# Side products in the banks of the score pairs, in an attention and block-quantized feed-forward kernel

## The chip, the cores and the metric

The kernel runs on one core of one Trainium2 chip. The metric is the device time of one execution in microseconds (us). The core has five engines, each with a queue of its own that it works off in order: TensorE (PE; its weight loads are listed apart as PEld), VectorE (DVE), ScalarE (ACT), GpSimd (POOL) and SyncE (SP), which here only starts DMAs. TensorE writes its results into PSUM[...], and ScalarE or VectorE read them from there.

## The reference

`x` is 4 x 1024 x 256, the context is 4 x 77 x 256, both float32. One attention block and one feed-forward block, each with a layer norm ahead and a residual around it:

```python
# attention: 16 heads of 16; keys and values from the context followed by x itself
q = x @ Wq
xc = concatenate((mem, x), axis=1)
k, v = split(xc @ Wkv, 2, axis=-1)
dots = einsum('bhid,bhjd->bhij', q, k) * scale
mask = j_idx > i_idx + mem_len            # causal behind the 77 context keys
attn = softmax(where(mask, -inf, dots), axis=-1)
out = einsum('bhij,bhjd->bhid', attn, v) @ Wout + bout
# feed-forward: both operands of both products rounded in blocks of 32
def block_quant(v):                       # exponent from the block's largest magnitude, 3 bits
    e = floor(log2(max(amax, tiny)))
    scale = exp2(e - 3)
    return round(vb / scale) * scale
h = gelu(einsum('bsk,nk->bsn', block_quant(x), block_quant(w_fc)) + b_fc)    # 1024 hidden
y = einsum('bsk,nk->bsn', block_quant(h), block_quant(w_proj)) + b_proj
# whole
x = x + attention(layernorm(x), ctx);  x = x + feed_forward(layernorm(x))
```

## The kernel before

**Groups, steps and half steps.** The 4 batches have 16 heads, taken in groups of 4, so there are 16 groups (`kk`). For one group the scores are computed twice. The first time gives, for each query row, the maximum over its keys (`max_matmul`, L451, then `max_reduce` on DVE, L475 or L477). The maxima are carried by DMA into a spare row of the queries, so that the second time the product is the score less its maximum (`score_matmul`, L515). The exponential on ACT (`score_exp`, L526) reads it from PSUM and writes `pt`; POOL clears what the causal mask forbids (L531), and `times_v` (L552) multiplies by V, summing into one bank of its own.

The maxima of group `kk + 1` run beside the scores of group `kk`. A group has 14 pieces (key tile by query stretch of up to 512), each done in two half steps for two heads each. A half step (`half_step`) issues on PE: maximum of head 1, score of head 1, maximum of head 2, score of head 2. These lie in four different row groups of the PE array, 32 rows each. The text calls the two maxima of a half step the first and the second. Then come two reductions on DVE and one exponential for the pair of scores on ACT. `times_v` follows for a piece two steps back, four matmuls for each half step. There are 448 half steps, and ahead of them 14 steps (`first_step`) in which the maxima of group 0 are computed alone, four heads at a time.

**Side work.** All else is cut into units which `run` puts between the half steps: layer norm and transposes of the next batch (`norm_unit`, L324; `mem_unit`, L343), projections to V (`v_unit`, L359) and to Q and K (`qk_unit`, L386), output product of attention (`wout_unit`, L642 and its bias L646), the two feed-forward products with their transposes (`in_unit`, L683; `hidden_unit`, L702 and L707; `out_unit`, L736, L744 and L747), and the quantized weights, transposed (`weight_unit`, L771). Each unit has a cost written by hand; `run` spreads the sum of the costs over the half steps and begins a unit when its share is due. Its later stages come some half steps after. The order of all instructions is fixed in this way when the program is built (`tc.manual_schedule()`); the engines keep to it and wait for each other by semaphores.

A side product, as the text uses the word, is one PSUM tile written by one of these units other than `hidden_unit`. ACT reads most of them (copies); the two output products (L642, L744) are read by DVE, which adds them to the residual (L647, L748). There are 256 of them, 198 of them after 75 us and before 1067 us.

**PSUM.** Tiles of a pool take its slots in turn, in order of allocation. A tile's first write waits until the last read of the tile that had its slot before has ended.

```python
ps_st = ap("ps_st", 2, space=PSUM)   # score pairs: 2 slots of two banks
ps_av = ap("ps_av", 1, space=PSUM)   # products with V: 1 bank
ps_s = ap("ps_s", 3, space=PSUM)     # s_tile: 3 banks
```

Score pairs (both scores of a half step, one tile) and the hidden products take `ps_st`; maxima and side products take `ps_s` together through `s_tile`. In `first_step` two of four maxima take `ps_s`, the other two a pair of `ps_st`.

**Ahead and behind.** Until about 75 us the first batch is normed and projected and group 0's maxima are found. From there to 1067 us the half steps run. After that come the last batch's output product (its second half) and its feed-forward, with no scores beside them.

Of the kernel before, what the change touches and what calls it, by code (L numbers as in the profile page):

```python
# [9 lines left out]
F32 = mybir.dt.float32  # L10
# [33 lines left out]
def kernel(  # L44
# [158 lines left out]
    with ExitStack() as actx:  # L203
# [52 lines left out]
        def s_tile(shape, dtype=F32):  # L256
            return ps_s.tile(shape, dtype, tag="s", name="s_ps")

        xT, o_pk, sums = {}, {}, {}


# [42 lines left out]
        def norm_unit(b, it):  # L304
            t = b * NT + it
            got = {}

            def scale_rows():
                held["xh"] += 1
                xh = work.tile([P, D], F32, name="xh")  # L310
                nc.vector.tensor_scalar(
                    xh, xn[b, it // HN][:, it % HN, :], mv1[:, t, 0:1], rstd1[:, t : t + 1],
                    ALU.subtract, ALU.mult,
                )
                got["xh"] = xh

            def turn():
                if it == 0:

                    assert b == 0 or projected[b - 1] == 2 * KC  # L320
                    xT[b] = xtp.tile([P, KC, KEYS], F32, name="xT")
                tp = s_tile([P, KC, P])
                for k in range(KC):
                    nc.tensor.transpose(tp[:, k, :], got["xh"][:, k * P : (k + 1) * P], ident)  # L324
                held["xh"] -= 1
                nc.scalar.copy(xT[b][:, :, M + it * P : M + (it + 1) * P], tp)
                normed[b] += 1

            scale_rows.ready = room("xh", XH)
            return cost(0.8, [scale_rows, turn])  # L330

        def mem_unit(b):
            got = {}

            def fetch():
                held["xh"] += 1
                got["m"] = work.tile([P, D], F32, name="xh")
                nc.sync.dma_start(out=got["m"][:M, :], in_=mem[b])

            def turn():  # L340
                tp = s_tile([P, KC, M])
                for k in range(KC):
                    nc.tensor.transpose(  # L343
                        tp[:, k, :], got["m"][:M, k * P : (k + 1) * P], ident[0:M, 0:M]
                    )
                held["xh"] -= 1
                nc.scalar.copy(xT[b][:, :, 0:M], tp)  # L347
                normed[b] += 1

            fetch.ready = room("xh", XH)  # L350
            return cost(0.5, [fetch, turn])

        def v_unit(b, jt):
            def emit():
                assert normed[b] == NT + 1
                nj = min(P, KEYS - jt * P)
                vp = s_tile([P, D])
                for k in range(KC):
                    nc.tensor.matmul(  # L359
                        vp[:nj, :], xT[b][:, k, jt * P : jt * P + nj], wv[:, k, :],  # L360
                        start=(k == 0), stop=(k == KC - 1),
                    )
                base = vaugs[b % 2][:nj, jt, :]
                nc.scalar.copy(
                    bass.AP(
                        base.tensor, base.offset,
                        [base.ap[0], [VP, HPC], [VOFF[1], 2], [2, HD]],
                    ),
                    vp[:nj, :].rearrange("p (q e d) -> p q e d", e=2, d=HD),
                )  # L370
            return emit

        def qk_unit(hh, which, part):

            def emit():
                b, hi = divmod(hh, KC)
                assert normed[b] == NT + 1
                if which == "q":
                    w, first, total = wq_sb, M, N
                else:  # L380
                    w, first, total = wk_sb, 0, KEYS
                lo = part * ICW
                n = min(ICW, total - lo)
                pp = s_tile([P, ICW])
                for k in range(KC):
                    nc.tensor.matmul(  # L386
                        pp[:, :n],
                        w[:, k, hi * P : (hi + 1) * P],
                        xT[b][:, k, first + lo : first + lo + n],
                        start=(k == 0),  # L390
                        stop=(k == KC - 1),
                    )
                nc.scalar.copy(qk_st[:, lo : lo + n], pp[:, :n])  # L393
                projected[b] += lo + n == total
            return cost(1.0, emit)
# [235 lines left out]
        def wout_unit(b, it):  # L631
            t = b * NT + it
            ic = it * P // ICW

            def fetch():
                x2[t] = xrp.tile([P, D], F32, name="x2")
                nc.sync.dma_start(out=x2[t], in_=xf[t * P : (t + 1) * P, :])

            def project():
                yp = s_tile([P, D])  # L640
                for k in range(KC):
                    nc.tensor.matmul(  # L642
                        yp, o_pk[b, ic][:, k, it * P % ICW : it * P % ICW + P], wo_sb[:, k, :],
                        start=(k == 0), stop=False,
                    )
                nc.tensor.matmul(yp, ones3, bias3[:, B_OUT : B_OUT + D], start=False, stop=True)  # L646
                nc.vector.tensor_add(x2[t], x2[t], yp)  # L647
                stats(x2[t], mv2, t)
                done["wout"] += 1

            fetch.ready = lambda: (b, ic) in divided and len(x2) - done["out"] < X2
            return cost(1.8, [fetch, project])
# [14 lines left out]
        def in_unit(t):  # L667
            got = {}

            def quantize():  # L670
                done["begun"] += 1
                held["xq"] += 1
                xh = work.tile([P, D], F32, name="xh")
                nc.vector.tensor_scalar(
                    xh, x2[t], mv2[:, t, 0:1], rstd2[:, t : t + 1], ALU.subtract, ALU.mult
                )
                got["xq"] = ffn.tile([P, D], BF16, name="xq", bufs=XQ)
                quant_round(xh, quant_steps(xh, D, "x"), got["xq"])

            def turn():  # L680
                tp = s_tile([P, KC, P], BF16)
                for k in range(KC):
                    nc.tensor.transpose(tp[:, k, :], got["xq"][:, k * P : (k + 1) * P], identb)  # L683
                held["xq"] -= 1
                xqT[t] = ffn.tile([P, KC, P], BF16, name="xqT", bufs=HBUF + 1)
                nc.scalar.copy(xqT[t], tp)  # L686

            quantize.ready = lambda: (
                t // HN in rooted and done["begun"] - len(hs) <= HBUF
                and held["xq"] < XQ and held["xh"] < XH  # L690
            )
            return cost(1.6, [quantize, turn])

        def hidden_unit(tiles):


            def emit():
                for t in tiles:
                    hp = ps_st.tile([P, 2, ICW], F32, name="st_ps")
                    for n in range(HID // ICW):  # L700
                        for k in range(KC):
                            nc.tensor.matmul(  # L702
                                hp[:, n, :], xqT[t][:, k, :],
                                wfcT[:, k, n * ICW : (n + 1) * ICW],
                                start=(k == 0), stop=False,
                            )
                        nc.tensor.matmul(  # L707
                            hp[:, n, :], ones3,
                            bias3[:, B_FC + n * ICW : B_FC + (n + 1) * ICW],
                            start=False, stop=True,  # L710
                        )
                    hs[t] = hp_.tile([P, HID], F32, name="h")
                    nc.scalar.activation(  # L713
                        hs[t], hp.rearrange("p e n -> p (e n)"), AF.Gelu
                    )
# [5 lines left out]
        def out_unit(t):  # L721
# [9 lines left out]
                done["round"] += 1  # L731

            def turn():
                tp = s_tile([P, HC, P], BF16)
                for k in range(HC):
                    nc.tensor.transpose(tp[:, k, :], got["hq"][:, k * P : (k + 1) * P], identb)  # L736
                held["hq"] -= 1
# [1 line left out]
                nc.scalar.copy(got["hT"], tp)  # L739

            def project():
                yp = s_tile([P, D])
                for k in range(HC):
                    nc.tensor.matmul(  # L744
                        yp, got["hT"][:, k, :], wprT[:, k, :], start=(k == 0), stop=False
# [10 lines left out]
        def weight_unit(src, into):  # L756
# [9 lines left out]
                quant_round(got["w"], quant_steps(got["w"], D, "x"), got["wb"])  # L766

            def turn():
                tp = s_tile([P, KC, P], BF16)
                for k in range(KC):  # L770
                    nc.tensor.transpose(tp[:, k, :], got["wb"][:, k * P : (k + 1) * P], identb)  # L771
                held["xq"] -= 1
# [48 lines left out]

        def first_step(n):

            st = ps_st.tile([P, 2, ICW], F32, name="st_ps")
            tops = [s_tile([P, ICW]), s_tile([P, ICW]), st[:, 0, :], st[:, 1, :]]
            for c, sp in enumerate(tops):
                max_matmul(0, MAXP[n], c, sp)
# [3 lines left out]
        def half_step(kk, n, pair):  # L831
# [2 lines left out]
            tops, st = [], None  # L834
            has_max, has_main = kk + 1 < B * NG, kk >= 0
            if has_main:
                st = ps_st.tile([P, 2, ICW], F32, name="st_ps")
            for e in range(2):
                if has_max:
                    tops.append(s_tile([P, ICW]))  # L840
# [150 lines left out]
```

## Time and profile before

| | us |
|---|---|
| median of 3 runs | 1178.98 (1171.74 to 1199.69) |
| profiled execution | 1168.32 |
| its span, first to last instruction | 1166.6 |
| PE busy | 1040.3 |
| DVE busy | 767.3 |
| ACT busy | 515.5 |
| POOL busy | 224.2 |

The mean granted clock of TensorE in the profiled execution is 0.902 of full speed. Busy times overlap, since the engines run at the same time. A line of the waits names the engine, the tile and source line that waited, then what released it, then the total in us, the number of times and the longest. A line of the timeline has its start, its duration, the engine, the source line, the operation with output and input tiles, and in brackets how long the engine had stood idle and what ended that. A row by stage has the stretch, its length, busy time and count of instructions for PE, PEld, DVE, ACT and POOL, the granted clock, the DMA engines' share and the GB/s. Every fp32 matmul of L451 and L515 appears as two records with the same source line.

### The profile page before, as it was taken

The numbers are of one execution on the slowest core, as the hardware profiler recorded it, in microseconds if no ns is written. First come the engines' busy times: TensorE is split into PE (matmuls) and PEld (weight loads), VectorE is DVE, ScalarE is ACT, GpSimd is POOL, SyncE is SP. The second block draws the span as 40 slices with busy tenths as digits, with TensorE's granted clock in tenths as the row PEclk, the third lists the DMA queues.
The fourth block names the chain that finished last, engine by engine and source line by source line (L and its number), as shares of the span: only waits on it lengthen the run. The fifth ranks groups of instructions, "written<-read, shape, count | busy, mean of one in ns | idle before, by whom it ended". The sixth has DMA issues, their size and how long they took to land.

```text
span 1166.6 us, 20970 instructions
## 1 busy us (share of the span) xinstructions
PE 1040.3 (89%) x8014; PEld 431.9 (37%) x8024; DVE 767.3 (66%) x2410; ACT 515.5 (44%) x720; POOL 224.2 (19%) x419
## 2 busy tenths in 40 slices
PE   2799999999988899999988899999999799999665
PEld 1353334343423234344423324434444233343222
DVE  8686776665677576477568646657667686652764
ACT  2123455555433454555334254555444454663212
POOL 3000212021101122031101103112211122151312
PEclk9887999999978898999979669999999898998565
DMA  2121001101310001100320001010112000002100
GB/s 76 39 67 26 18 26 35 40 16 32 102 37 14 6 6 31 35 12 29 94 57 2 13 6 28 19 25 22 49 39 51 6 12 11 15 21 62 25 23 19
DMA packets 36118, 36.35 MB, mean 31 GB/s; under 512 B 14005, under 2 KB 29679, under 8 KB 36018
## 3 DMA queue, kind: packets, MB, share of 16 engines
q1 hardware_dynamic: 34912, 33.95, 10.8%
q8 instruction: 63, 1.03, 0.4%
q10 hardware_dynamic: 1106, 1.07, 0.3%
q14 instruction: 37, 0.30, 0.1%
HBM read 16.59 MB, written 5.24 MB: 19 GB/s over the span
## 4 chain that ended last, share of the span: by engine, by line
PE 67%; DVE 22%; issue 3%; DMA 3%; ACT 2%; SPq 1%; POOL 1%; POOLq 0%; DVEq 0%; ACTq 0%
PE s_ps L451 30%; PE av_ps L552 13%; PE s_ps L386 5%; PE st_ps L515 4%; DVE jk L477 4%; DVE mx L475 3%; PE st_ps L702 3%; PE s_ps L642 3%; DVE amaxh L171 2%; PE s_ps L359 2%; PE s_ps L744 2%; PE st_ps L707 2%; DVE h L191 1%; PE s_ps L736 1%; DVE st L145 1%
## 5 line engine op out<-in xcount | busy, mean ns | idle before, releaser
L451 PE MATMUL s_ps<-kT,qT 32*128 32x512 f32 (+2 forms) x1736 | 528.6, 564 | 58.0 <-DVE mxp L477 25.7
L526 ACT ACTIVATE pt<-st_ps 128x1024 f32<-128x1024 f32 (+4 forms) x448 | 355.0, 794 | 413.3 <-PE st_ps L515 388.5
L515 PE MATMUL st_ps<-qT,kT 32*128 32x512 f32 (+5 forms) x1792 | 531.1, 559 | 0.2 <-ACT pt L526 0.2
L451 PEld LDWEIGHTS s_ps<-kT,qT 32*128 32x128 f32 x1736 | 204.6, 194 | 251.8 <-DVE mxp L477 71.0
L531 POOL TENSOR_SCALAR_AFFINE_SELECT pt<-pt 128x254 f32<-128x254 f32 (+3 forms) x320 | 123.2, 386 | 616.7 <-ACT pt L526 616.6
L477 DVE CUSTOM_DVE_ANT_0 jk<-s_ps,tri,mx 128x77 bf16<-128x77 f32 (+3 forms) x372 | 173.0, 504 | 100.2 <-PE st_ps L515 73.9
L552 PE MATMUL av_ps<-pt,vaug 128*32 128x256 f32 (+7 forms) x3072 | 231.1, 374 | 7.2 <-POOL pt L531 4.1
L475 DVE TENSOR_REDUCE mx<-s_ps 128x1 f32<-128x512 f32 x248 | 159.6, 684 | 115.2 <-PE st_ps L515 92.1
L515 PEld LDWEIGHTS st_ps<-qT,kT 32*128 32x128 f32 (+1 forms) x1792 | 200.9, 190 | 14.6 <-issue 9.2
L477 DVE CUSTOM_DVE_ANT_0 jk<-s_ps,tri 128x512 bf16<-128x512 f32 (+3 forms) x248 | 126.4, 548 | 62.1 <-PE st_ps L515 49.6
L552 PEld LDWEIGHTS av_ps<-pt,vaug 128*32 128x32 f32 (+1 forms) x3072 | 62.3, 110 | 215.4 <-issue 166.9
L192 POOL TENSOR_TENSOR hq<-h,magh 128x1024 bf16<-128x1024 f32 x32 | 61.2, 1912 | 181.9 <-DVE h L191 181.9
L393 ACT COPY qk_st<-s_ps 128x512 f32<-128x512 f32 (+1 forms) x40 | 20.3, 513 | 73.7 <-PE s_ps L386 69.1
L713 ACT ACTIVATE h<-st_ps 128x1024 f32<-128x1024 f32 x32 | 32.6, 1023 | 38.5 <-PE st_ps L707 38.4
L702 PE MATMUL st_ps<-wfcT,xqT 128*128 128x512 bf16 x118 | 45.2, 464 | 4.6 <-ACT xqT L686 3.1
L739 ACT COPY hT<-s_ps 128x1024 bf16<-128x1024 bf16 x32 | 32.4, 1012 | 35.2 <-PE s_ps L736 34.9
L642 PE MATMUL s_ps<-wo_sb,o_pk 128*128 128x256 f32 x128 | 41.5, 450 | 2.3 <-DVE o_pk L620 2.0
L748 DVE TENSOR_TENSOR x<-x,s_ps 128x256 f32<-128x256 f32 x32 | 13.3, 415 | 45.0 <-PE s_ps L747 44.9
L171 DVE TENSOR_REDUCE amaxh<-h 128x32 f32<-128x1024 f32 x32 | 38.6, 1207 | 5.8 <-ACT h L713 5.7
L477 DVE DVE_READ_ACCUMULATOR2_ANT mxp<- 128x1 f32 x512 | 41.9, 82 | 0.0
L744 PE MATMUL s_ps<-wprT,hT 128*128 128x256 bf16 x256 | 39.4, 305 | 1.2 <-ACT hT L739 1.2
L386 PE MATMUL s_ps<-xT,wk_sb 128*128 128x512 f32 (+1 forms) x96 | 39.6, 545 | 0.4 <-ACT xT L347 0.4
(90 smaller groups left out, 767.0 us busy)
## 6 DMA issues: line engine op xcount, KB each, us to landing
kT<-qk_st SPq DMA_DIRECT2D x16, 275.2 KB
xn<-in_x_dram SPq DMA_DIRECT2D x16, 256.0 KB
qT<-qk_st SPq DMA_DIRECT2D x16, 256.0 KB
o_pk<-o_st SPq DMA_DIRECT2D x32, 128.0 KB
rb<-rd SPq DMA_DIRECT2D x128, 32.0 KB
x<-in_x_dram SPq DMA_DIRECT2D x32, 128.0 KB
out_dram<-x SPq DMA_DIRECT2D x32, 128.0 KB
x<-in_L_ffn_w_fc_dram SPq DMA_DIRECT2D x8, 128.0 KB
```

The costliest lines, as they stand in the source:

```text
L171: nc.vector.tensor_reduce(amax, src.rearrange("p (n k) -> p n k", k=QBLK), axis=AX.X, op=ALU.max, apply_absolute_value=True,)
L386: nc.tensor.matmul(pp[:, :n], w[:, k, hi * P : (hi + 1) * P], xT[b][:, k, first + lo : first + lo + n], start=(k == 0), stop=(k == KC - 1),)
L451: nc.tensor.matmul(sp[:, 0 : hi - lo], qTs[kk % NQK][rows, it * P : (it + 1) * P], kTs[kk % NQK][rows, lo:hi], start=True, stop=True,)
L475: nc.vector.tensor_reduce(into, sp[:, 0:w], axis=AX.X, op=ALU.max)
L477: nc.vector.tensor_tensor_reduce(junk.tile([P, ICW], BF16, name="jk")[:, 0:w], sp[:, 0:w], mask, 1.0, before, ALU.add, ALU.max, into)
L515: nc.tensor.matmul(st[:nj, e, : i1 - i0], kTs[kk % NQK][rows, t * P : t * P + nj], qTs[kk % NQK][rows, i0:i1], start=True, stop=True,)
L526: nc.scalar.activation(pt[:nj, :, :w], st[:nj, :, :w], AF.Exp, scale=scale)
L531: nc.gpsimd.affine_select(out=pt[:nj, :, :behind], in_=pt[:nj, :, :behind], compare_op=ALU.is_ge, fill=0.0, base=base, pattern=[[0, 2], [1 ...
L552: nc.tensor.matmul(acc[c * PAD : (c + 1) * PAD, off + lo : off + hi], vaugs[b % 2][:nj, t, v0 : v0 + PAD], pts[kk, n, c // 2][:nj, c % 2, ...
L642: nc.tensor.matmul(yp, o_pk[b, ic][:, k, it * P % ICW : it * P % ICW + P], wo_sb[:, k, :], start=(k == 0), stop=False,)
L702: nc.tensor.matmul(hp[:, n, :], xqT[t][:, k, :], wfcT[:, k, n * ICW : (n + 1) * ICW], start=(k == 0), stop=False,)
L744: nc.tensor.matmul(yp, got["hT"][:, k, :], wprT[:, k, :], start=(k == 0), stop=False)
```

## The change

A new helper takes a tile of the pool `ps_st` under the same tag as the score pairs, so a side product takes one of their two slots, in turn with them. All side products use it in place of `s_tile`; the maxima keep `s_tile` and its three banks. The score pairs and hidden products name the tag explicitly, since it must be the same. Nothing else is changed; the lines behind the helper move down by four.

```diff
         def s_tile(shape, dtype=F32):
             return ps_s.tile(shape, dtype, tag="s", name="s_ps")
 
+        def side_tile(shape, dtype=F32):
+
+            return ps_st.tile(shape, dtype, tag="st", name="side_ps")
+
...
-                tp = s_tile([P, KC, P])
+                tp = side_tile([P, KC, P])
...
-                tp = s_tile([P, KC, M])
+                tp = side_tile([P, KC, M])
...
-                vp = s_tile([P, D])
+                vp = side_tile([P, D])
...
-                pp = s_tile([P, ICW])
+                pp = side_tile([P, ICW])
...
-                yp = s_tile([P, D])
+                yp = side_tile([P, D])
...
-                tp = s_tile([P, KC, P], BF16)
+                tp = side_tile([P, KC, P], BF16)
...
-                    hp = ps_st.tile([P, 2, ICW], F32, name="st_ps")
+                    hp = ps_st.tile([P, 2, ICW], F32, tag="st", name="st_ps")
...
-                tp = s_tile([P, HC, P], BF16)
+                tp = side_tile([P, HC, P], BF16)
...
-                yp = s_tile([P, D])
+                yp = side_tile([P, D])
...
-                tp = s_tile([P, KC, P], BF16)
+                tp = side_tile([P, KC, P], BF16)
...
-            st = ps_st.tile([P, 2, ICW], F32, name="st_ps")
+            st = ps_st.tile([P, 2, ICW], F32, tag="st", name="st_ps")
...
-                st = ps_st.tile([P, 2, ICW], F32, name="st_ps")
+                st = ps_st.tile([P, 2, ICW], F32, tag="st", name="st_ps")
```

## The prediction

> **What bounds the kernel now.** I read the page first, for the share of each engine.
>
> ```profile
> PE 1040.3 (89%) x8014; PEld 431.9 (37%) x8024; DVE 767.3 (66%) x2410; ACT 515.5 (44%) x720; POOL 224.2 (19%) x419
> ```
>
> TensorE (PE) is busy for 89% of 1166.6 us, so what is worth anything is time in which PE stands or runs half filled. Then the waits, for what PE stands on; PEld, its weight loads, sees a wait before the running matmul has ended.
>
> ```profile
> PEld s_ps L451 <- DVE mxp L477: 71.0, 132, 5.4
> PEld s_ps L451 <- DVE mx L475: 50.6, 76, 3.7
> PEld s_ps L451 <- DVE mx L477: 28.5, 45, 3.0
> ...
> PEld st_ps L515 <- ACT pt L526: 3.7, 9, 0.5
> ```
>
> The maxima's matmuls (L451) waited 150 us in all, 253 times, for a reduction on VectorE (DVE) to free one of their three banks. The scores (L515) waited 3.7 us for the exponential on ScalarE (ACT). So the score pairs have room and the maxima have none. Third, the timeline, for what one such wait is. Around 426 us, in time order, with start, duration, engine:
>
> ```profile
> 425.17 0.73 ACT L526 ACTIVATE pt<-st_ps 128x666 f32<-128x666 f32 x1 [1.18 <-PE st_ps L515]
> ...
> 425.53 0.28 PE L683 MATMUL s_ps<-identb,xq 128*128 128x128 bf16 x2
> ...
> 426.33 0.56 DVE L477 CUSTOM_DVE_ANT_0 jk<-s_ps,tri,mx 128x333 bf16<-128x333 f32 x1
> ...
> 426.95 0.54 PE L451 MATMUL s_ps<-kT,qT 32*128 32x333 f32 x1 [1.14 <-DVE mxp L477]
> ...
> 426.96 0.54 PE L515 MATMUL st_ps<-qT,kT 32*128 32x333 f32 x1
> ```
>
> A side product (L683) took the third bank, so the next maximum needs the bank of the half step just before, and stands 1.14 us until its reduction ends. But the same view elsewhere shows what stands in the pairs' way:
>
> ```profile
> 144.40 0.94 ACT L526 ACTIVATE pt<-st_ps 128x922 f32<-128x922 f32 x1 [0.25 <-PE st_ps L515]
> ...
> 144.47 0.29 PE L771 MATMUL s_ps<-identb,xq 128*128 128x128 bf16 x2
> ...
> 144.69 0.65 PE L515 MATMUL st_ps<-qT,kT 32*128 32x461 f32 x1
> ...
> 145.23 0.37 ACT L773 COPY wfcT<-s_ps 128x256 bf16<-128x256 bf16 x1
> ```
>
> The next score starts at 144.69, while the exponential of the last score runs until 145.34. Now these are different slots. With the side product in one of the two pair slots, that score must write where the exponential still reads.
>
> [...] from 425.8 to 426.95 no PE matmul runs, though the score at 426.96 had its bank free. [...] Here both rings rotate; the trace shows 150 us where three banks aren't enough and 3.7 us where two pairs are.
>
> **The change part by part.** In the built program no instruction is added, removed or moved on any of the five engines, DMA issues included: all five queues hold the same work in the same order. Only banks change, and with them waits. Slots go round in order of allocation: the maxima keep three banks to themselves; scores, hidden products and sides share two pairs. Four terms, all from the instruction times in the trace of before, comparing each write's start with the end of the read that frees its new slot (0.06 us from such an end to the released matmul, the smallest gap of the waits shown).
>
> *Relief of the maxima.* Between 75 and 1067 us, 216 maxima start within 0.2 us of the release of their bank. Their gap on PE beyond the usual gap for the same neighbour is 58.8 us. 178 of them, with 43.5 us, are second maxima of a half step. These wait for the first maximum of the half step before, and in the new ring nearly all have the same predecessor: relief 1.1 us. 38 are first maxima, all but a few of them after a side: 15.3 us, and all would go. But the second maximum of such a half step then inherits the reduction that the first one waited for (426.95 above; the second starts at 427.44), so at most some 0.5 us a time stays: at the level of the second maximum 6.9 us are left.
>
> *New wait of the scores.* A score right after one side waits for the exponential just issued. Its end against the score's present start:
>
> | side before it | scores | late | us |
> |---|---|---|---|
> | L771, L683 (bf16 turns) | 31 | 21 | 7.5 |
> | L324, L736 (turns) | 42 | 22 | 4.7 |
> | L359, L386 (projections) | 49 | 6 | 0.8 |
> | L642, L744 (output products) | 33 | 5 | 2.8 |
> | others, a side further back | 293 | 18 | 1.3 |
>
> Together 17.0 us, in 72 of 448 half steps. The long sides cover it: an L386 has two matmuls of 0.59 us. The short ones don't: 0.3 us of turns against an exponential of 0.94 to 1.02. Queued behind the waiting score on PE are the second pair of matmuls, four products with V (L552) and the next side; waiting for these are the two reductions on DVE and the next exponential. Taken with the relief at the same place, the second maxima start 12.8 us later in sum in 419 half steps that have both, and in the last group, which has no maxima, 1.6 us come on top.
>
> *Waits of the sides.* Sides lose 2.5 us of waits for reductions. They gain 1.1 us for the slot before last; hidden products gain 0.8. A side's eviction on ACT stands behind the exponential, but has a half step until its slot is wanted. One on DVE (L647, L748) stands behind two reductions; its late cases are the 2.8 us of the table.
>
> Sum for the main part: 12.8 + 1.6 - 6.9 - 2.5 + 1.1 + 0.8 = +6.9 us. About a quarter of the maxima wait for DVE anyway, and a delay of PE just ahead of one is swallowed there; I keep three quarters, +5.
>
> *Head and tail.* Sides have two slots where they had three. After 1067 us, PE is busy 63.5 of 100 us:
>
> ```profile
> 1067.00:1167.00 100.00, 63.49 (x256) 28.07 (x252) 57.40 (x136) 20.65 (x27) 21.42 (x18) 0.59 0.10 30
> ```
>
> Of 40 writes there five would be late, by 2.8 us; the chain goes through DVE and POOL between them, so I take 1.5, from 0 to 2.8 and, if a delay is handed on to each later tile, 10. Before 75 us 17 of 38 writes would be late, 7.6 us in sum; there the reductions set the pace (four for each step) and the projections stand beside them, and the transposes wait for DVE in any case. I take 1.0, from 0 to 3; less than nothing is possible too, since the maxima of this part also lose the sides from their ring: down to -2.
>
> In all +7.5 us. The profiled execution took 1168.3 us, with 1166.6 of span and 1.7 around it: 1176 by the trace. The runs shown are 1171.7, 1179.0 and 1199.7, so that execution is 0.9% below their median. I put the sum on the middle of both, 1173.7: **1181 us**, no change that can be told. About 2%, 23 us, is what a measurement of this kernel can tell from none.
>
> **The rivals.** *The exponential takes the reduction's place* (forecast, 0.58): 1181. For it: 72 late exponentials in the trace, against 38 relieved waits of which at most 0.5 us each stays. *The relief wins* (0.18): all 15.3 + 2.5 us are kept and half of 18.9 is swallowed in the second maxima's waits: -8, 1165. For it: 43.5 us of DVE waits stand ready to swallow. Against: those at 426.95 and the like are handed to the next matmul. *DVE works ahead* (0.05): with three banks of its own half of the 43.5 us go as well, -25 with the relief and few losses, 1149, faster by 2%. Against: the second maximum's predecessor is the same tile as before. *The score chain becomes the bound* (0.13), slower: after a short side the period is scores 1.15, exponential 1.02 and two handovers of 0.1, about 2.3 us, before the next score, where PE alone needs 1.15 + 0.57 + 0.3 (scores and products with V as the timeline has them at 412 us). Each delay of the second maximum by DVE then delays exponential and next score together, and nothing of the relief is left. At 0.3 us more on each of the 73 short sides +22 comes to the 7.5: 1203. It decides from about 0.25 us more per short side, on top of the 0.17 (12.2 over 73) read above. For it: the median of such scores is within 0.3 us of being late, so small shifts make most of them late. *The tail* (0.06): each of the last eight tiles is handed a delay, +10 with the rest, 1191. That the change doesn't separate the rings is excluded by the built program's banks.
>
> **How the numbers follow.** Forecast, relief and tail lie within 2%: 0.82. Score chain slower: 0.13. DVE ahead faster: 0.05. The upper bound of the unknown terms is no relief at all, 17.0 + 1.9 + 3 + 2.8 = +25, 1199; the lower is the relief's -8, with some -2 of the head, 1163. The range of 1163 to 1200 leaves out the faster case and half of the slower one.
>
> **What would show it.** Scores (L515) waiting for pt L526 where there were 3.7 us: 10 to 20 us in the weight loads, mostly after turns. L451's waits for DVE down from 150 us by 10 to 25, those of the second maximum unchanged. Tail length 100 us within 3. Busy times of DVE, ACT and POOL the same within 1%. I would be wrong if L515's wait exceeded 35 us, if L451's fell by half, or if the tail grew by more than 5.

## The result, and the profile after

The kernel after took 1191.3 us (median of 4 executions, 1190.8 to 1193.9), the kernel before 1175.7 us (median of 4). The ratio is 1.0142, with a 95% interval of 1.0108 to 1.0175: slower by 1.4%, under the 2% that the forecast's chances went by, but told apart from no change. A ratio leaves out executions more than 1.5% above the fastest of their kernel, while medians and means here take all, so it is not their quotient. The forecast was 1181 us, in a range of 1163 to 1200.

The profiled execution of the kernel after took 1193.9 us with a span of 1192.2. Its page, first part; the lines of the maxima are L455, of the scores L519, of the reductions L479 and L481, of the exponential L530, four below those of before:

```profile
PE 1066.1 (89%) x8014; PEld 443.5 (37%) x8024; DVE 768.8 (64%) x2410; ACT 515.8 (43%) x720; POOL 224.8 (19%) x419
```

DVE, ACT and POOL do what they did, within 0.3%, and in the order of before, instruction for instruction (2410, 720 and 419 of them). PE's busy time has grown by 25.8 us, as much as the span (25.6 us), though not an instruction was added to it. That is the first sign of where the time went. The waits of PE's weight loads in the kernel after (before, for the maximum at 426.95, the weight load had stood 1.31 us and the matmul 1.14):

```profile
PEld s_ps L455 <- DVE mxp L481: 72.0, 128, 5.4
...
PEld s_ps L455 <- DVE mx L479: 45.0, 60, 3.7
PEld s_ps L455 <- DVE mx L481: 27.6, 39, 3.3
...
PEld st_ps L519 <- ACT pt L530: 10.7, 24, 0.8
...
PEld st_ps L519 <- ACT hT L743: 1.4, 3, 0.6
...
PEld st_ps L519 <- DVE x L752: 1.3, 3, 0.5
PEld st_ps L519 <- DVE x L651: 1.2, 1, 1.2
```

The maxima wait 144.6 us in place of 150.1. The scores wait 10.7 us for the exponential in place of 3.7, and 3.9 for evictions of side products, where it was 0.4. The maxima's waits for the evictions of side products, some 13 us before (L326, L347, L364, L393, L647, L739, L748, L773), are down to 1.3. All in all the waits shown did not grow, and do not make up the 16 us. The two places that the prediction showed, now in the timeline of the kernel after; first the relieved one:

```profile
434.37 0.73 ACT L530 ACTIVATE pt<-st_ps 128x666 f32<-128x666 f32 x1 [1.79 <-PE st_ps L519]
...
434.74 0.28 PE L687 MATMUL side_ps<-identb,xq 128*128 128x128 bf16 x2
...
434.95 0.54 PE L455 MATMUL s_ps<-kT,qT 32*128 32x333 f32 x1
...
435.15 0.54 PE L519 MATMUL st_ps<-qT,kT 32*128 32x333 f32 x1
...
436.16 0.54 PE L455 MATMUL s_ps<-kT,qT 32*128 32x333 f32 x1 [0.19 <-DVE mxp L481]
```

The first maximum follows its side product at once. The second one, 1.42 us after the start of the side product, waits for the reduction that the first one waited for before; there it was 1.91 us. So 0.5 us are won of 1.14. Then the place of the new wait:

```profile
142.82 0.94 ACT L530 ACTIVATE pt<-st_ps 128x922 f32<-128x922 f32 x1 [0.17 <-PE st_ps L519]
...
142.89 0.28 PE L775 MATMUL side_ps<-identb,xq 128*128 128x128 bf16 x2
...
143.11 1.04 PE L455 MATMUL s_ps<-kT,qT 32*128 32x461 f32 x2
...
143.81 0.65 PE L519 MATMUL st_ps<-qT,kT 32*128 32x461 f32 x1
```

The score starts 0.92 us after its side product, where it was 0.22: the exponential (142.82 to 143.76) is in its way, by 0.70 us, as reckoned from the trace of before (0.65 and 0.06 for the release).

By stage (columns as named under the profile before), first the kernel before, then the kernel after: up to the first half step, the half steps, and the tail.

```profile
0.00:74.80 74.80, 45.12 (x199) 22.84 (x199) 55.83 (x156) 14.04 (x29) 11.65 (x19) 0.95 0.24 68
74.80:1066.70 991.90, 931.38 (x7566) 380.74 (x7573) 653.86 (x2119) 480.51 (x664) 190.86 (x383) 0.93 0.11 28
1066.70:1166.60 99.90, 63.79 (x260) 28.34 (x264) 57.57 (x137) 20.90 (x27) 21.72 (x18) 0.59 0.10 30
```

```profile
0.00:78.30 78.30, 45.98 (x199) 21.82 (x199) 55.71 (x156) 14.02 (x29) 11.65 (x19) 0.96 0.23 65
78.30:1090.20 1011.90, 956.06 (x7563) 393.22 (x7567) 655.42 (x2119) 480.71 (x664) 191.71 (x383) 0.91 0.10 28
1090.20:1192.20 102.00, 64.07 (x262) 28.43 (x264) 57.66 (x137) 21.11 (x27) 21.40 (x18) 0.58 0.11 30
```

The head is 3.5 us longer, the tail 2.1, the half steps 20.0. In these the granted clock fell from 0.93 to 0.91. These two traces record the clock as 1.00 or as 0.50, which the text calls full and half. Between first and last score PE ran at half clock for 139 us before, in 12 spells of 3.4 to 30.7 us, and for 188 us after, in 16 spells of the same range. I put each of the 448 half steps beside its counterpart: some 380 that ran at full clock in both traces take the same in sum, within 2 us. Some 20 that were at half clock only in the kernel after are 21 to 24 us longer. (The figures depend a little on where a half step is taken to begin.) Half of the 20 us lies in one stretch, about group 5; kernel before, then kernel after:

```profile
350.00:440.00 90.00, 79.08 (x606) 32.52 (x603) 61.65 (x221) 39.91 (x62) 16.12 (x35) 0.91 0.04 12
```

```profile
348.50:449.40 100.90, 92.25 (x606) 35.86 (x603) 62.25 (x222) 39.89 (x62) 16.26 (x35) 0.78 0.04 10
```

The same 606 matmul records took 10.9 us more, at a clock of 0.78 in place of 0.91. That does not make this stretch the change's: group 5 has 17 us at half clock in this trace of the kernel before and 44 in the kernel after, but 41 in a second trace of the kernel before (below).

### The profile page after: what moved, and what is told of

The parts are those of the page before. It is cut to its first block, busy times and chain, and to the rows that moved or that the text cites. A ratio compares the mean times of both kernels' runs of the same rounds, so it can differ in the third digit from the quotient of the medians.

```text
span 1192.2 us, 20958 instructions
## 1 busy us (share of the span) xinstructions
PE 1066.1 (89%) x8014; PEld 443.5 (37%) x8024; DVE 768.8 (64%) x2410; ACT 515.8 (43%) x720; POOL 224.8 (19%) x419
## 3 DMA queue, kind: packets, MB, share of 16 engines
q8 instruction: 63, 1.03, 0.4%
## 4 chain that ended last, share of the span: by engine, by line
PE 68%; DVE 21%; issue 3%; DMA 3%; ACT 2%; SPq 1%; POOL 1%; POOLq 0%; DVEq 0%; ACTq 0%
PE s_ps L455 27%; PE av_ps L556 13%; PE st_ps L519 6%; PE side_ps L390 5%; DVE jk L481 5%; PE st_ps L706 3%; PE side_ps L646 3%; DVE mx L479 2%; PE side_ps L363 2%; PE st_ps L711 2%; PE side_ps L748 2%; DVE amaxh L171 2%; DVE h L191 1%; PE side_ps L740 1%; ACT pt L530 1%
## 5 line engine op out<-in xcount | busy, mean ns | idle before, releaser
L455 PE MATMUL s_ps<-kT,qT 32*128 32x512 f32 (+2 forms) x1736 | 537.1, 567 | 50.6 <-DVE mxp L481 25.2
L530 ACT ACTIVATE pt<-st_ps 128x1024 f32<-128x1024 f32 (+4 forms) x448 | 355.3, 794 | 421.7 <-PE st_ps L519 397.2
L519 PE MATMUL st_ps<-qT,kT 32*128 32x512 f32 (+5 forms) x1792 | 524.8, 565 | 2.1 <-DVE x L651 1.1
L455 PEld LDWEIGHTS s_ps<-kT,qT 32*128 32x128 f32 x1736 | 208.1, 196 | 235.9 <-DVE mxp L481 72.0
L481 DVE CUSTOM_DVE_ANT_0 jk<-s_ps,tri,mx 128x77 bf16<-128x77 f32 (+3 forms) x372 | 173.2, 505 | 104.3 <-PE st_ps L519 69.8
L479 DVE TENSOR_REDUCE mx<-s_ps 128x1 f32<-128x512 f32 x248 | 160.2, 685 | 121.1 <-PE st_ps L519 69.8
L519 PEld LDWEIGHTS st_ps<-qT,kT 32*128 32x128 f32 (+1 forms) x1792 | 193.4, 193 | 25.9 <-ACT pt L530 10.7
L481 DVE CUSTOM_DVE_ANT_0 jk<-s_ps,tri 128x512 bf16<-128x512 f32 (+3 forms) x248 | 127.2, 549 | 66.7 <-PE st_ps L519 49.6
L397 ACT COPY qk_st<-side_ps 128x512 f32<-128x512 f32 (+1 forms) x40 | 20.4, 514 | 78.1 <-PE side_ps L390 71.8
L706 PE MATMUL st_ps<-wfcT,xqT 128*128 128x512 bf16 x118 | 48.3, 493 | 3.9 <-ACT pt L530 2.3
L743 ACT COPY hT<-side_ps 128x1024 bf16<-128x1024 bf16 x32 | 32.4, 1012 | 37.2 <-PE side_ps L740 37.0
L752 DVE TENSOR_TENSOR x<-x,side_ps 128x256 f32<-128x256 f32 x32 | 13.3, 416 | 51.0 <-PE side_ps L751 51.0
L646 PE MATMUL side_ps<-wo_sb,o_pk 128*128 128x256 f32 x128 | 43.5, 469 | 2.4 <-DVE o_pk L624 2.1
L481 DVE DVE_READ_ACCUMULATOR2_ANT mxp<- 128x1 f32 x512 | 42.1, 82 | 0.0
L363 PE MATMUL side_ps<-wv,xT 128*128 128x256 f32 (+1 forms) x144 | 39.0, 400 | 2.3 <-ACT vaug L368 1.4
L390 PE MATMUL side_ps<-xT,wk_sb 128*128 128x512 f32 (+1 forms) x96 | 38.8, 536 | 2.1 <-DVE mxp L481 1.3
```

Of the source, the lines that this page charges most:

```text
L363: nc.tensor.matmul(vp[:nj, :], xT[b][:, k, jt * P : jt * P + nj], wv[:, k, :], start=(k == 0), stop=(k == KC - 1),)
L390: nc.tensor.matmul(pp[:, :n], w[:, k, hi * P : (hi + 1) * P], xT[b][:, k, first + lo : first + lo + n], start=(k == 0), stop=(k == KC - 1),)
L455: nc.tensor.matmul(sp[:, 0 : hi - lo], qTs[kk % NQK][rows, it * P : (it + 1) * P], kTs[kk % NQK][rows, lo:hi], start=True, stop=True,)
L479: nc.vector.tensor_reduce(into, sp[:, 0:w], axis=AX.X, op=ALU.max)
L481: nc.vector.tensor_tensor_reduce(junk.tile([P, ICW], BF16, name="jk")[:, 0:w], sp[:, 0:w], mask, 1.0, before, ALU.add, ALU.max, into)
L519: nc.tensor.matmul(st[:nj, e, : i1 - i0], kTs[kk % NQK][rows, t * P : t * P + nj], qTs[kk % NQK][rows, i0:i1], start=True, stop=True,)
```

## How far time follows the clock

Each execution comes with its mean granted clock. The 132 executions of the kernel before that ran with the experiments below lie from 1160 to 1197 us, on a line: us = 2048.6 - 973.9 x clock. The spread about it is 1.6 us (standard deviation), where that of the times is 7.6. Put in other terms, 1 us more at half clock costs 0.38 us (with the clock at 1.00 or 0.50, the time at half clock is twice the time, times one less the mean clock). So a kernel's time can be split: what its mean clock would give the kernel before, and the rest, which is its cost at equal clock. In us, against the kernel before's means of 1176.2 us and 0.8959:

| kernel | executions | mean us | clock | by the clock | at equal clock |
|---|---|---|---|---|---|
| after, both series | 8 | 1191.9 | 0.8872 | +8.4 | +7.3 |
| head left as before | 20 | 1188.0 | 0.8877 | +7.9 | +3.9 |
| feed-forward transposes left as before | 12 | 1177.3 | 0.8991 | -3.1 | +4.2 |
| norm and context transposes left as before | 4 | 1190.6 | 0.8885 | +7.2 | +7.2 |
| transposes only | 20 | 1180.8 | 0.8898 | +5.9 | -1.3 |
| norm and context transposes only | 20 | 1175.5 | 0.8949 | +0.9 | -1.6 |
| projections and output products only | 11 | 1179.2 | 0.8952 | +0.7 | +2.4 |
| after, maxima first behind a side product | 16 | 1187.7 | 0.8915 | +4.2 | +7.3 |
| after, each transpose twice | 20 | 1180.9 | 0.9150 | -18.6 | +23.3 |
| before, inverse deviation in stages | 4 | 1153.1 | 0.9055 | -9.4 | -13.7 |
| after, inverse deviation in stages | 4 | 1159.4 | 0.9042 | -8.2 | -8.7 |

The line is that of the kernel before; for kernels with other work it is a reckoning, not a measurement. The executions of the kernels with the change lie on flatter lines of their own (the 20 with the head left: 748 us in place of 974); with that slope the kernel after would have 6.5 us by the clock and 9.2 at equal clock, so the two columns are sure only to some 2 us.

## The experiments

**The kernel before once more.** No edit.

> The kernel before, once more, for a second trace and the granted clock of several executions. Waits theory (the cost of the change is the time that scores stand for the exponential): about 1173 us, and nothing of interest in the clock. Clock theory (the direct waits of the change net to nothing, and the 16 us are TensorE at half clock for longer): about 1173 us with a mean clock of 0.90 or more in every execution, and about 140 us at half clock between the first and the last score. Accident theory (how long the clock stays down after a gap is a matter of chance and has nothing to do with the change): clocks from 0.88 to 0.905 in different executions, times from 1170 to 1200 along with them.

Measured: 1175.7 us (median of 12), ratio 1.0006 (0.9979 to 1.0033). The clock went from 0.881 to above 0.90, and the time with it. The execution that was traced took 1191.5 us; its half steps, where the first trace has 991.90 us:

```profile
74.70:1084.10 1009.40, 947.55 (x7572) 385.32 (x7573) 654.09 (x2119) 481.24 (x664) 190.75 (x383) 0.91 0.10 28
```

So the accident theory is right for single executions: two traces of the kernel before lie over 20 us apart, and a difference between two traces proves little here. Whether the lower clock belongs to the change takes means over executions.

**The kernel after once more.** No edit; run later, for that question.

> The kernel after, once more. Clock theory (the change costs some 4 to 7 us at equal clock, and the rest of its 16 us is TensorE at half clock, because after the idle gaps of the groups 5 and 9 the clock stays down for 30 us each time): mean clock 0.883 to 0.891 in all executions, 1188 to 1194 us, and 44 us at half clock in each of the groups 5 and 9. Accident theory (the four executions of the kernel after were a chance draw): clocks up to 0.90, and times down to 1178 us.

Measured: 1191.9 us (1187.8 to 1196.1), ratio 1.0112 (1.0025 to 1.0198), clocks 0.882 to 0.893. All eight executions of the kernel after lie between 0.882 and 0.893, with a mean of 0.8872 against 0.8959. The lower clock belongs to the change.

**Transposes only, and the long sides only.** From the kernel after, `side_tile` is turned back into `s_tile` in some places:

```diff
-                vp = side_tile([P, D])
+                vp = s_tile([P, D])
-                pp = side_tile([P, ICW])
+                pp = s_tile([P, ICW])
-                yp = side_tile([P, D])
+                yp = s_tile([P, D])
```

This is the kernel with the transposes only (`yp` stands in two places). For the long sides only, it is the five `tp` that are turned back:

```diff
-                tp = side_tile([P, KC, P])
+                tp = s_tile([P, KC, P])
...
-                tp = side_tile([P, HC, P], BF16)
+                tp = s_tile([P, HC, P], BF16)
```

> Only the transposes (the short sides) take slots of the score pairs; projections and output products stay with the maxima. Waits theory: 12.2 of the 17.0 us of late exponentials lie behind these, and less of the relief comes along, so 1185 to 1192 us. Clock theory: if the extra time at half clock comes from the scores' waits behind short sides, 1185 to 1192 with a clock below 0.89 and 180 us or more at half clock. Accident theory: anything from 1170 to 1195.

> Only projections and output products (the long sides) take slots of the score pairs; transposes stay with the maxima. Waits theory: late exponentials of 3.6 us against a relief of some 3.5 us of the first maxima, so 1170 to 1178 us. Clock theory: the same, 1170 to 1178, with the clock back at 0.90 and some 140 us at half clock. Accident theory: anything from 1170 to 1195.

Measured: transposes only 1.0062 (1.0037 to 1.0086), 1179.7 us; long sides only 1.0011 (0.9967 to 1.0056), 1180.2. Neither is the 1.4% of both together. The transposes came out below the range of both the waits and the clock theory, the long sides 2 us above theirs. At equal clock the transposes cost nothing (-1.3 us), though 12.2 of the 17.0 us of late exponentials lie behind them. In their trace the scores wait 5.0 us more for the exponential and 1.4 more for evictions, and 6.0 us of waits of maxima for the transposes' evictions are gone; that one makes up for the other is likely. What they cost is clock, 5.9 us. The waits theory falls for them. At equal clock the two halves make 1.1 us (-1.3 and +2.4), and both together cost 7.3; why they don't add up is open.

**Each transpose twice.** In the kernel after:

```diff
-                for k in range(KC):
+                for k in [*range(KC)] * 2:
                     nc.tensor.transpose(...)
```

and likewise for the range over `HC`; the second pass writes the same values again.

> The kernel after, with every transpose issued twice into the same tile, so that there is PE work where the score would stand for the exponential (about 0.15 to 0.5 us for each of 110 turns, some 25 us of matmuls in all). Waits theory: what is added behind a turn takes the place of the wait, some 12 us are covered, so about 1191 + 13 = 1204 us. Clock theory: more work on PE shortens the time at half clock too, so 1185 to 1197 us, with less than 187 us at half clock between the first and the last score. Accident theory: 1195 to 1225.

Measured: 1180.3 us (median of 20), mean clock 0.915, ratio to before 1.0061 (1.0029 to 1.0092). That is below the range of every theory. With more work on PE it is 11 us *faster* in the mean than the kernel after: by the line, 16 us more at equal clock and 27 us less by the clock. Its trace has 126 us at half clock between the scores in place of 188, and is 10.0 us shorter in the half steps and 3.0 in the tail. The waits theory had the added work make it slower, 1204 us; what moved the other way is the granted clock, from 0.8872 to 0.9150. How much of the change's own 16 us is clock this run does not tell.

**The gap of group 5.** In the middle of the groups 5 and 9 PE stands idle until DVE, behind 14 small instructions of an inverse deviation (2.8 us) and a quantization, gets to the reduction that the next maximum waits for. Two transposes just ahead no longer wait for each other's eviction in the kernel after, so PE arrives sooner and the gap is 4.0 us in place of the 3.25 of the kernel before:

```profile
387.15 0.49 PE L451 MATMUL s_ps<-kT,qT 32*128 32x77 f32 x1 [3.25 <-DVE mxp L477]
```

I took that for what sends the clock down, and moved all but these transposes, or these alone:

```diff
-                tp = side_tile([P, KC, P])
+                tp = s_tile([P, KC, P])
-                tp = side_tile([P, KC, M])
+                tp = s_tile([P, KC, M])
```

This is all but these, from the kernel after. In the other kernel `side_tile` stays in these two lines and is `s_tile` everywhere else.

> The kernel after, with the transposes of the normed rows and of the context (two lines) back among the maxima's banks. Gap theory (two of these in a row no longer wait for each other, PE comes 0.75 us sooner to a maximum that waits for the chain of the inverse deviation on DVE, the idle gap there grows from 3.25 to 4.0 us, and the clock stays down for longer after it): the gap is 3.25 again, half clock in the main part 140 to 175 us, 1172 to 1180 us. Even theory (each side product adds a little, by the scores' waits for the exponential): these transposes have 2.2 of the 17.0 us of late exponentials, so 1184 to 1191 us.

> The kernel before, with these two lines alone moved to the slots of the score pairs. Gap theory: gaps of 4.0 us in the groups 5 and 9, spells of about 30 us at half clock behind them, 1179 to 1188 us with a mean clock of about 0.888. Even theory: 1173 to 1178 us with the clock of before, 0.897.

Measured: without them 1190.3 us, 1.0133 (1.0080 to 1.0187); they alone 1175.6 us, 0.9995 (0.9966 to 1.0024). The gap did what was expected of it, in the timeline of the kernel with these two alone:

```profile
384.26 0.44 PE L519 MATMUL st_ps<-qT,kT 32*128 32x77 f32 x2
388.74 0.49 PE L455 MATMUL s_ps<-kT,qT 32*128 32x77 f32 x1 [4.03 <-DVE mxp L481]
```

but the time did not change. This theory falls: the longer gap does not cost the 16 us. Nor does it decide how long the clock stays down behind it: the spell lasts 30.7 us in this trace, and with the short gap 10.2 us in the first trace of the kernel before and 30.7 in the second.

**The inverse deviation in stages.** The gap theory's other test, on both kernels: the seed and each of the three Newton steps become a stage of their own, one half step apart.

```diff
-    def inv_std(mv, rstd, t0, t1):
-        ...
-        for step in range(3):
-            ...
+    def inv_std(mv, rstd, t0, t1):
+        ...
+        return [seed] + [(1, newton(i)) for i in range(3)]
...
-                if i + 2 == HN:
-                    inv_std(mv1, rstd1, b * NT + half * HN, b * NT + (half + 1) * HN)
-            return cost(1.5, emit)
+            stages = [emit]
+            if i + 2 == HN:
+                steps = inv_std(mv1, rstd1, b * NT + half * HN, b * NT + (half + 1) * HN)
+                stages += [(1, steps[0])] + steps[1:] + [(0, lambda: rooted1.add((b, half)))]
+            return cost(1.5, stages)
...
-            emit.ready = lambda: done["wout"] >= b * NT + (half + 1) * HN
-            return cost(1.5, emit)
+            steps[0].ready = lambda: done["wout"] >= b * NT + (half + 1) * HN
+            return cost(1.5, steps + [(0, lambda: rooted.add(b * NT // HN + half))])
```

`norm_unit` also waits for `rooted1`.

> The kernel before, with the 14 instructions of each inverse deviation on DVE, 2.8 us without a break, cut into four stages that are issued one half step apart. Gap theory: the idle gaps of 2.3 to 4.9 us on PE in the groups 0, 4, 5, 8, 9 and 13 shrink below 2 us, half clock in the main part falls from 140 to 175 us to less than 90, and the time to 1140 to 1158 us. Even theory: only the idle time itself goes, at most some 12 us: 1162 to 1170 us, with the clock of before.

> The kernel after, with the same cut of the inverse deviation. Gap theory: with the gaps gone what the change costs goes too: within 6 us of the kernel before with the same cut. Even theory: the 16 us between before and after stay.

Measured: the kernel before with it 1151.2 us, 0.9769 (0.9684 to 0.9853), which beats both kernels; the kernel after with it 1159.2 us, 0.9853 (0.9788 to 0.9918). PE's waits in the first of these:

```profile
PE s_ps L464 <- DVE mxp L490: 18.0, 28, 2.5
PE s_ps L747 <- POOL hq L200: 16.2, 6, 6.1
PE s_ps L464 <- DVE mx L488: 8.1, 15, 1.3
```

The longest wait of a maximum for DVE is 2.5 us in place of 4.8. The times are as the gap theory had them, but not for its reason: half clock between the scores was still 129 us, not below 90, and of the 23 us won some 14 are at equal clock and 9 by the clock. The two kernels lie 8 us apart in the medians and 6 in the means, from four executions each, and their intervals overlap: whether the change costs less here stays open.

**The head.** In the kernel after, sides keep `s_tile` until the first score:

```diff
+        scoring = []
+
         def side_tile(shape, dtype=F32):
+            if not scoring:
+                return s_tile(shape, dtype)
             return ps_st.tile(shape, dtype, tag="st", name="side_ps")
...
+        scoring.append(True)
         for kk in range(last + 1):
```

> The kernel after, with the side products before the first score (transposes and projections of the first batch, V and the second K) left among the maxima's banks. If the head is where the cost at equal clock lies: first score at 74.7 us again where the kernel after has it at 78.3, and 1185 to 1189 us with the clock of after, 0.887. If not: 1189 to 1194 us.

Measured: 1188.4 us (median of 20), ratio 1.0133 (1.0103 to 1.0164). Up to the first half step, where the kernel after has 78.30:

```profile
0.00:75.80 75.80, 46.22 (x199) 23.41 (x199) 55.78 (x156) 14.04 (x29) 11.65 (x19) 0.93 0.24 67
```

At nearly the same mean clock (0.8877 and 0.8872) it is 3.9 us below the kernel after. The head costs 3.4 us at equal clock (7.3 - 3.9). Which side products do it, the traces of the two partial kernels show; transposes only, then projections and output products only:

```profile
0.00:74.30 74.30, 45.28 (x198) 22.12 (x198) 55.79 (x156) 14.05 (x29) 11.67 (x19) 0.95 0.24 69
0.00:79.50 79.50, 46.81 (x199) 22.82 (x199) 55.98 (x156) 14.03 (x29) 11.67 (x19) 0.96 0.22 64
```

It is the projections. Those to V wait for their own evictions, from 40 us to the first half step, in the kernel before and in the kernel after:

```profile
PEld s_ps L359 <- ACT vaug L364: 2.2, 3, 0.8
PEld side_ps L363 <- ACT vaug L368: 4.8, 6, 0.9
```

**The feed-forward's transposes.** Back to `s_tile` in the kernel after, in `in_unit` and `out_unit`:

```diff
-                tp = side_tile([P, KC, P], BF16)
+                tp = s_tile([P, KC, P], BF16)
...
-                tp = side_tile([P, HC, P], BF16)
+                tp = s_tile([P, HC, P], BF16)
```

> The kernel after, with the two transposes of the feed-forward (of the quantized rows and of the quantized hidden values) left among the maxima's banks. Clock theory, if the scores' waits behind these transposes are what keeps the clock down in the groups 5 and 9: mean clock 0.894 to 0.898, less than 75 us at half clock in these two groups together where the kernel after has 89, and 1178 to 1184 us. If something else keeps it down: 0.887 and 1187 to 1193 us.

Measured: 1178.3 us (median of 12), ratio 1.0045 (1.0005 to 1.0085), clock 0.8991. These two lines carry 14.6 of the change's 15.7 us in the means: 11.5 by the clock, 3.1 at equal clock. The place is not the expected one. In its one trace the groups 5 and 9 have 85 us at half clock together, against 89 in the kernel after; what is gone are spells of 3 to 10 us in the groups 6, 8, 10, 11 and 15, together 14 us where the kernel after has 48.

**Maxima first.** In the kernel after, in half steps behind a side product (`side_tile` now notes each tile in `sided`):

```diff
+            behind = bool(sided) and has_main
+            sided.clear()
             for e in range(2):
                 if has_max:
                     ...
-                if has_main:
+                if has_main and not behind:
                     score_matmul(kk, n, other * 2 + e, st, e)
+            for e in range(2):
+                if behind:
+                    score_matmul(kk, n, other * 2 + e, st, e)
```

> The kernel after; in a half step that follows a side product both maxima are issued first and both scores behind them, so that the second maximum's matmul stands where PE would wait for the exponential. Waits theory: the 12 us of late exponentials behind short sides shrink to some 4, 1180 to 1187 us. Clock theory: with the waits the clock recovers too, 0.893 or more, 1174 to 1184 us. Against both: the second maximum waits for DVE more often than the score for ACT, and the pair of scores now stands behind that wait, 1190 to 1198 us.

Measured: 1186.7 us (median of 16), ratio 1.0155 (1.0127 to 1.0183). The scores' wait for the exponential halved, from 10.7 to 5.2 us:

```profile
PEld st_ps L521 <- ACT pt L532: 5.2, 16, 0.5
```

but the maxima's wait for the reductions rose as much, from 144.6 to 150.2 us:

```profile
PEld s_ps L457 <- DVE mxp L483: 75.2, 132, 5.4
...
PEld s_ps L457 <- DVE mx L481: 45.7, 58, 3.7
PEld s_ps L457 <- DVE mx L483: 29.3, 38, 4.2
```

The waits changed places, as the third case had it, and the cost at equal clock stayed at 7.3 us. The median lies in the range of the waits theory, but by the line the 4 us that the mean is lower are all clock; the clock, 0.8915, missed the clock theory's 0.893. Inconclusive: since the waits did not go, this run neither clears nor convicts them.

## Why the prediction was right, and where it was not

The outcome lay in the range and in the case that had 0.82: slower, by less than 2%. It was not "no change that can be told": the interval, 1.0108 to 1.0175, leaves out 1. The parts of its sum fared differently.

- **Relief of the maxima: right in kind, smaller.** The first maximum is freed and the second inherits the wait, with 0.5 us won at the place shown. The waits for reductions fell by 5.5 us; 10 to 25 were expected. Some 12 us of waits of maxima for evictions of side products went besides, which the list of signs did not have.
- **New wait of the scores: right.** 10 to 20 us at L519 were expected; it is 10.7 for the exponential, 14.6 with the evictions.
- **Main part, +5: too high.** In the trace the half steps take 20.0 us more, with 48.4 us more at half clock. The executions of the kernel before give 0.38 us for each us at half clock, so 18.5 of the 20.0 are clock and 1.5 are left. The half steps of that kernel's two traces give 0.47 (17.5 us for 37.6), by which 2.5 us less than nothing is left. At full clock in both traces they differ by less than 2 us. So the new waits and the relief about cancel, where three quarters of 6.9 us were to be left.
- **Head, +1.0, up to 3.** Mis-sized: 3.5 us, confirmed by leaving the head alone. I had read 7.6 us of late writes there and put most of them beside the reductions' pace. That "the projections stand beside them" was the wrong part: with two slots shared with the maxima of `first_step` they are what waits (4.8 us in place of 2.2 for the evictions of V).
- **Tail, +1.5.** 2.1 us in the two traces, which shows nothing: the second trace of the kernel before has a tail of 105.6 us, longer than either.
- **Sum.** The split by the line gives 7.3 us at equal clock; forecast were 7.5. That it fits this well is luck: the main part was too high and the head too low, the tail can't be told, and the split itself is sure only to some 2 us.
- **What failed: a term that was not there.** The sum was made on the durations of one execution with a granted clock of 0.902 and added to 1173.7 us, as if the kernel after would be granted the same clock as the kernel before. It was granted 0.887 in the mean, worth 8.4 us, more than all that I had reckoned with. None of the rivals held it either. The upper end of the range was set for other causes; that it held is luck.

The rival of the score chain (1203 us, 0.3 us more for each short side) is refuted at its size: the scores wait 10.7 us for the exponential where it needed 22 us more behind short sides, and transposes alone cost nothing at equal clock. That DVE works ahead was right not to be expected: of 150.1 us of waits for reductions 144.6 are left.

What stays open is how the two feed-forward transposes bring the clock down. That they do is shown by their removal (0.8991 against 0.8872) and, in part, by transposes only against norm and context transposes only (0.8898 against 0.8949). What it is about them that does it was not shown: more matmuls in these places raised the clock to 0.915, but doubled transposes add work behind every transpose and do not single these two out. Open too is where the 4 us at equal clock lie that are not the head's: the feed-forward transposes carry 3.1 of them here, and all transposes together cost nothing where they moved without the long sides.

## What to carry to other kernels

Where PE is the bound and its granted clock varies, look at the clock first, in many executions: take the slope of time against clock from repeats of one kernel, and split every difference into clock and the rest, before explaining it by waits. A wait that is taken away from a first instruction may only move to the next one that needs the same release (at the place shown 0.5 us of 1.14 were won); reckon the relief at the second. And small instructions in a chain on another engine, here 14 on DVE, can be worth more than the banks: cutting them into stages gave 2.3% (1.5 to 3.2, from four executions).

## What the runs showed of the hardware that was not expected

The kernel before runs between 1160 and 1197 us, and 96% of that variance follows the mean granted clock (9.7 us for 0.01). Issuing each transpose twice sped the kernel after up: 1191.9 to 1180.9 us in the mean, with the mean clock at 0.9150 in place of 0.8872. And 13.8 us of a busy PE passed before the clock came back: in group 5 of the kernel after PE was busy without a break from 403.8 us, first with the hidden products (L706, L711), and stayed at half clock until 417.6 us. The rows by stage show it in the third column from the end; the matmuls' durations agree, two of L706 taking 1.03 us where two of L702 took 0.60 in the kernel before:

```profile
406.00:410.00 4.00, 4.00 (x9) 0.55 (x7) 0.00 (x0) 1.93 (x2) 0.00 (x0) 0.50 0.00 0
410.00:414.00 4.00, 4.00 (x9) 0.58 (x8) 0.00 (x0) 1.02 (x1) 0.00 (x0) 0.50 0.00 0
```
